# Attention scores for 512 queries and one key block at a time, in a fused Mamba and attention kernel

## The chip, the cores and the metric

The kernel runs on one core of a Trainium2 chip. The metric is the device time of one execution in microseconds. The core has five engines, each with an instruction queue of its own that runs in order: TensorE (PE; its weight loads are shown apart as PEld), VectorE (DVE), ScalarE (ACT), GpSimd (POOL) and SyncE (SP), which here issues the DMAs. Matmuls write into PSUM, which has eight banks of 512 f32 values in each of 128 partitions. GpSimd does not read PSUM in this kernel.

## The reference, cut to what matters

A conditioned state-space layer comes first and its result is added to x; then attention follows on x of shape (4, 1024, 512) with 16 heads of 32 channels. The change lies in the attention:

```python
q = heads(jnp.einsum('bsh,oh->bso', x, q_weight) * q_dc[:, None, :])
k = heads(jnp.einsum('bsh,oh->bso', x, k_weight) * k_dc[:, None, :])
v_flat = jnp.einsum('bsh,oh->bso', x, v_weight) * v_dc[:, None, :] * s2[:, None, :]
skip = v_flat
v = heads(v_flat)
attn = jnp.einsum('bhqd,bhkd->bhqk', q, k) * scale
attn = jax.nn.softmax(attn, axis=-1)
out = jnp.einsum('bhqk,bhkd->bhqd', attn, v).transpose(0, 2, 1, 3).reshape(B, S, H)
out = jnp.einsum('bsh,oh->bso', out, w_weight) * w_dc[:, None, :]
skip = jnp.einsum('bsh,oh->bso', skip, u_weight) * u_dc[:, None, :]
return out + skip
```

For every batch, head and query there are 1024 scores; their exponentials are summed (the denominator) and weight the values (the numerator), and the quotient goes through two projections.

## The kernel before

The state-space layer fills the first 1365 us of the span and the attention the rest. Attention is cut into 32 units (`NU`, line 1094): four batches, four groups of four heads, two halves of 512 queries. All 1024 keys of a unit's four heads lie in `ks` and its 512 queries in `qs`, with a 97th row that carries the negated maximum of each query's scores, so that the score matmul gives a number that can go straight into the exponential.

Work is written as small generators ("threads"), and `Loom` (line 44) is a planner: it keeps a clock for each engine, and each `yield` names an engine, an estimated duration and conditions. Whoever can start first is written next, with ties broken by a rank. The order it finds is fixed in each engine's queue by `Lane` (line 157). So the planner's estimates decide the order, and the chip's real durations decide how long each engine stands still within it. `Bins` (line 125) hands out buffers in the plan.

The threads that matter here, in one unit:

- `scores` (line 1152) runs over two halves of 256 queries (`qq`), four pairs of key blocks (`kp`) and four heads (`h`). Each step takes one of two PSUM banks (`sts`) and writes two matmuls of 128 keys by 256 queries, one for each key block of the pair.
- `exponent` (line 1165) is one ScalarE instruction over 128 x 512 values, into one of 12 SBUF buffers `p` (`PB`).
- `sums` (line 1184) adds the four `p` of a head and a query half: three additions of 512 columns, then a fold that adds the 256 columns of the second key block to those of the first. Head 1 does it on VectorE (`VADD`), the other three on GpSimd. There are four buffers `s` (`SB`).
- `groups` (line 1230) forms outputs: two groups for each query half, each with 16 matmuls (four key blocks, four heads), K of 128 keys, 32 output channels, 256 queries. Four heads go side by side into four column tiles of the array (`tile_position`) and into the 128 partitions of one of two banks `avs`, of which the outputs use the first 256 columns.
- `pay` (line 1206) sums over the partitions: four matmuls with a matrix of ones over the `s` of the four heads, 256 columns, into the other 256 columns of the same bank. It is written inside the next output group, or by `alone` (line 1225) when the planner comes to that first; a group that opens a query half has `due` of the owed sums among its conditions. A payment frees the four `s` buffers.
- `ratio` (line 1263): VectorE's reciprocal of the sums, then its product with the outputs, 256 queries at a time, and a store to DRAM (`aod`).

Beside these, `peaks` and `peak` (lines 1317 and 1330) find the maxima for the next unit (`dps`, `r`, `mps`), `heads` projects q and k (`qps`), `values` v (`vps`), and `skip`, `output` and `ending` do the last projections (`ups`, `ops`). They share the four common banks (`bank_of`, line 1119). `ending` (line 1652) handles the last batch's last four token blocks: three quarters of the projection are formed ahead, and the last quarter when `final` is there, which `ratio` sets for each query half of the last unit.

Of the kernel before, what the change touches and what calls it, by code (L numbers as in the profile page):

```python
# [8 lines left out]
F32 = mybir.dt.float32  # L9
# [3 lines left out]
ALU = mybir.AluOpType  # L13
# [22 lines left out]
AFTER = mybir.DependencyInfo(mybir.DependencyClass.Sync, mybir.DependencyReason.DATA)  # L36
# [811 lines left out]
PB = 12  # L848
SB = 4
# [5 lines left out]
LAT1 = {'PE': 0.3, 'ACT': 0.4, 'DVE': 0.8, 'POOL': 0.8, 'SP': 4.0, 'L1': 0.0}  # L855
EXTRA = {'PE': 0.1, 'ACT': 0.3, 'DVE': 0.3, 'POOL': 0.5, 'SP': 1.0}
MARGIN = 0.9
END = (12, 3, 12)
LAND = {"q": 5.5, "k": 9.0, "d": 10.5}
DUE = {'norm': (-206, 14.4), 'heads': (-96, 24), 'v0': (-108, 2.2), 'v1': (12, 2.2), 'skip': (100, 8), 'out': (266, 9)}  # L860
# [229 lines left out]
def attention(ctx, E, T, out, begun):  # L1090
    tc, nc, I, dc, x1d = E.tc, E.nc, E.I, E.dc, E.x1d
    NT = T // 128
    U = 8
    NU = B * U
# [4 lines left out]
    pm, pst, pav = (ep(tc.tile_pool(name="l1" + n, bufs=c, space=PSUM, reuse_waits="tile"))  # L1099
                    for n, c in (("m", 1), ("st", 2), ("av", 2)))  # L1100
# [64 lines left out]
    def exponent(u, qq, kp, h, i, st):  # L1165
        key = u, qq, kp, h
        yield "ACT", 0.54, prs
        j = prs.take()
        p = work("p", [128, 2, 256], PB)
# [5 lines left out]
        if kp == 1:  # L1175
            loom.add(sums(u, qq, h), place(u, qq, 1, h))
# [7 lines left out]
    def sums(u, qq, h):  # L1184

        eng = "DVE+" if h in VADD else "POOL"
        us, add = (0.62, dve) if h in VADD else (1.3, pool)
        s = None
        for kp in range(1, 4):
            yield (eng, us) + ((srs,) if s is None else ()) + (have("p", u, qq, kp, h),)  # L1190
            first = s is None
            if first:
                j, s = srs.take(), work("s", [128, 2, 256], SB)
            add.tensor_tensor(out=s, in0=P[u, qq, 0, h][1] if first else s, in1=P[u, qq, kp, h][1], op=ALU.add)
            for x in (0, 1) if first else (kp,):
                drop((u, qq, x, h))
# [9 lines left out]
    def pay(u, qq):  # L1206

        a = owed.pop((u, qq))
        for h in range(4):
            sm = pe.matmul(a[1][32 * h:32 * h + 32, 1, :], ones, S[u, qq, h][1][:, 0, :], start=True, stop=True, tile_position=(0, 32 * h))  # L1210
            if h == 0:
                for x in range(1, 4):
                    tc.add_manual_dep(sm.ins, S[u, qq, x][2], AFTER, reason="heads together")
        for h in range(4):
            srs.give(S.pop((u, qq, h))[0])
        loom.add(ratio(u, qq, *a), place(u, qq, 3, 3))

    def due(u, qq):

        def at():  # L1220
            ts = [done.get(("sum", u, qq, h)) for h in range(4)]
            return 0.0 if (u, qq) not in owed else None if None in ts else max(ts) + MARGIN
        return at

    def alone(u, qq):
        yield "PE", 0.8, due(u, qq)
        if (u, qq) in owed:
            pay(u, qq)

    def groups():  # L1230

        v = E.v
        for u, qq, kg in np.ndindex(NU, 2, 2):
            hg = u % U // 2
            names = [(u, qq, kp, h) for kp in (2 * kg, 2 * kg + 1) for h in range(4)]
# [3 lines left out]
            vs = [have("v", u // U, hg // 2, tb) for tb in range(4 * kg, 4 * kg + 4)]  # L1239
            yield ("PE", 2.05 + (0.41 if kg == 0 and owed else 0.0), *conds, *vs)  # L1240
            if kg == 0:
                ai = avs_of.take()
                a = ai, pav.tile([128, 2, 256], F32, tag="a", name="avs")
            for i in range(4):
                kb = 4 * kg + i
                for h in range(4):
                    c = hg * 128 + 32 * h
                    mm = pe.matmul(a[1][32 * h:32 * h + 32, 0, :], v[:, kb, c:c + 32], P[u, qq, 2 * kg + i // 2, h][1][:, i % 2, :],
                                   start=kb == 0, stop=kb == NT - 1, tile_position=(0, 32 * h))
                    if i == 0 and h == 0:  # L1250
# [12 lines left out]
    def ratio(u, qq, ai, a):  # L1263
# [8 lines left out]
        mark("av1", u, qq)  # L1272
        if u == NU - 1:
            final[qq] = ao
            mark("final", qq)
            return
        yield "SP", 0.6
        sp.dma_start(out=aod[b, hg, :, qh * 512 + qq * 256:qh * 512 + qq * 256 + 256], in_=ao)
        aos.give(j)
        mark("ao", b, hg, 2 * qh + qq)  # L1280

# [247 lines left out]
    def values(b, hf):  # L1529
        yield "SP", 0.01, past("skip", b - 1)  # L1530
        j, (wh, wl) = yield from weight("v", b, hf)
        free = [past("av", b * U - 1 - 4 * (1 - hf), 1)]
        for tb in range(NT):
            i = None
            for half in range(2):
                yield ("PE", 0.75) + ((bank_of, have("xs", b, tb), *free) if i is None else ())
                if i is None:
                    i, ps = bank([128, 256], "vps")
                for kb in (2 * half, 2 * half + 1):
                    for n, (a, ww) in enumerate(((E.xh, wh), (E.xh, wl), (E.xl, wh))):  # L1540
                        pe.matmul(ps, a[:, kb, tb * 128:tb * 128 + 128], ww[:, kb, :], start=kb == 0 and n == 0, stop=kb == 3 and n == 2)
            yield "ACT", 0.3
            acte.copy(E.v[:, tb, hf * 256:hf * 256 + 256], ps)
            bank_of.give(i)
            mark("v", b, hf, tb)
        whs.give(j)
        mark("values", b, hf)
# [104 lines left out]
    def ending(b, tb):  # L1652
# [133 lines left out]
```

## Time and profile before

| | |
|---|---|
| median of 3 runs | 2790.56 us (2787.77 to 2792.78) |
| profiled execution | 2796.49 us |
| its span, first to last instruction | 2794.7 us |
| attention, 1365 to 2775 us: PE, DVE, ACT, POOL busy | 1328.4, 951.4, 961.7, 1118.6 us |
| mean granted TensorE clock | 0.951 |
| exponentials (p<-st), 1024 instructions | 606 ns each |
| reciprocals, 64 instructions of 256 columns | 1755 ns each |
| recorded rows of outputs (avs<-p) and sums (avs<-s) | 4096 and 512 |

Busy time of PE is the union of its matmuls' durations. A matmul's duration includes its way through the array, so two that follow each other overlap in the record, and what one costs the queue is the distance from its start to the next start. The weight loads are a track of their own, since they run under the matmul before. An f32 matmul of the text appears as two rows. The clock switches between 1.0 and 0.5 in short stretches. All attention instructions carry line 167, the helper `Lane`; they are told apart by their tiles: `st` scores, `p` exponentials, `s` partial sums, `avs` outputs and sums, `ao` the quotient.

### The profile page before, as it was taken

To read this page: it belongs to the slowest core of one execution; us is meant where nothing else is said; L and a number is where in the kernel's file an instruction comes from. 1 tells how busy PE (TensorE), PEld (TensorE's weight loads), DVE (VectorE), ACT (ScalarE), POOL (GpSimd) and SP (SyncE) were. 2 spreads that over 40 slices of the span, in tenths; PEclk is the share of its full clock that TensorE was granted. 3 is DMA by queue.
4 is the path that set the end of the run, shared out by engine and by line. 5 is a ranking of instruction groups with operands and counts; after the bars stand their busy time and mean duration, and the time that the engine had idled before them with its cause. 6 is when DMAs were issued, how large, how long until landed. Compare 5 with 4: busy or idle time off the path is not lost.

```text
span 2794.7 us, 54619 instructions
## 1 busy us (share of the span) xinstructions
PE 2566.8 (92%) x18421; PEld 1775.8 (64%) x18421; DVE 1994.9 (71%) x3518; ACT 2021.2 (72%) x3766; POOL 2083.1 (75%) x2365
## 2 busy tenths in 40 slices
PE   7798999999999998886989899989999899999998
PEld 7565565665566665433756677756777667777765
DVE  4778888888878887674557766677567786667665
ACT  5888888888888888663567677667766676676674
POOL 5887788787778787443378888787787787777786
PEclk9899999999999999787989999999999999999998
DMA  5789989999989999895652455344553545345422
GB/s 173 226 239 273 271 267 274 274 265 272 270 250 272 273 276 266 254 252 147 174 130 82 121 141 171 104 127 116 147 144 118 135 124 140 120 121 151 107 58 91
DMA packets 333772, 518.26 MB, mean 185 GB/s; under 512 B 33514, under 2 KB 108586, under 8 KB 333362
## 3 DMA queue, kind: packets, MB, share of 16 engines
q1 hardware_dynamic: 333076, 514.71, 65.1%
q8 instruction: 145, 2.38, 0.4%
q14 instruction: 135, 1.11, 0.1%
q10 hardware_dynamic: 416, 0.07, 0.0%
HBM read 422.35 MB, written 92.05 MB: 184 GB/s over the span
## 4 chain that ended last, share of the span: by engine, by line
PE 43%; DMA 15%; POOL 15%; ACT 11%; DVE 8%; issue 7%; SPq 0%; ACTq 0%; POOLq 0%; DVEq 0%
DMA rep<-xnd 9%; PE avs L167 8%; PE st L167 7%; POOL s L167 5%; ACT u L167 5%; PE ups L167 5%; PE qps L167 4%; DVE g L167 4%; PE mps L167 3%; PE ps L167 3%; POOL tmp L167 3%; PE vps L167 3%; PE dps L167 3%; POOL tm L167 2%; PE po L167 2%
## 5 line engine op out<-in xcount | busy, mean ns | idle before, releaser
L167 DVE CUSTOM_DVE_ANT_0 g<-g,u,hi 128x512 f32<-128x512 f32 x1024 | 820.5, 801 | 209.4 <-ACT u L167 171.3
L167 ACT ACTIVATE p<-st 128x512 f32<-128x512 f32 x1024 | 599.2, 606 | 312.3 <-PE st L167 288.6
L167 ACT ACTIVATE u<-rep,bd 128x512 f32<-128x512 f32 x1024 | 699.4, 689 | 121.5 <-DMA rep<-xnd 67.8
L167 POOL TENSOR_TENSOR s<-s,p 128x512 f32<-128x512 f32 x384 | 538.9, 1420 | 58.1 <-ACT p L167 57.2
L167 DVE CUSTOM_DVE_ANT_0 r<-mps,r 128x512 f32<-128x512 f32 x496 | 334.7, 683 | 271.9 <-PE mps L167 249.7
L167 PE MATMUL ps<-xh,w_in 128*128 128x256 f32 x2048 | 493.4, 317 | 15.2 <-ACT w_in L167 10.5
L167 PE MATMUL st<-qs,ks 97*128 97x256 f32 x2048 | 450.5, 305 | 33.1 <-ACT p L167 24.0
L167 PEld LDWEIGHTS st<-qs,ks 97*128 97x128 f32 x2048 | 350.1, 195 | 152.4 <-ACT p L167 82.8
L167 POOL TENSOR_TENSOR s<-p 128x512 f32<-128x512 f32 x192 | 255.1, 1342 | 202.2 <-PE avs L167 106.9
L167 PEld LDWEIGHTS ps<-xh,w_in 128*128 128x128 f32 x2048 | 344.8, 191 | 91.7 <-issue 65.3
L167 PE MATMUL yb<-g,sy 128*32 128x512 f32 x2048 | 287.9, 633 | 57.7 <-DVE g L167 42.5
L167 ACT ACTIVATE r<-dps 128x512 f32<-128x512 f32 x496 | 298.5, 606 | 42.2 <-DVE m L167 20.5
L167 POOL TENSOR_TENSOR tmp<-tmp,tm 128x256 f32<-128x256 f32 x372 | 272.6, 733 | 73.6 <-ACT tmp L167 44.6
L167 PE MATMUL ps<-xl,w_in 128*128 128x256 f32 x1024 | 290.2, 283 | 0.0
L167 PE MATMUL avs<-p,v 128*32 128x256 f32 x4096 | 269.8, 408 | 2.4 <-ACT p L167 2.3
L167 PE MATMUL mps<-ks,qs 96*128 96x512 f32 x528 | 222.3, 435 | 16.1 <-DMA ks<-bnc 9.7
L167 PEld LDWEIGHTS ps<-xl,w_in 128*128 128x128 f32 x1024 | 196.4, 192 | 30.1 <-issue 30.1
L167 PE MATMUL dps<-ds,qs 96*128 96x512 f32 x496 | 204.4, 413 | 11.6 <-DMA bnc<-fh 5.7
L167 PEld LDWEIGHTS avs<-p,v 128*32 128x32 f32 x4096 | 126.8, 116 | 112.6 <-issue 25.4
L167 POOL TENSOR_SCALAR tm<-xr,c_w_conv 128x256 f32<-128x256 f32 x372 | 182.3, 490 | 20.1
L167 PE MATMUL qps<-xs,wqh 128*128 128x512 f32 x480 | 190.1, 401 | 0.1
L167 PE MATMUL ups<-wo,th 128*128 128x256 f32 x960 | 187.8, 288 | 0.0
(389 smaller groups left out, 4826.2 us busy)
## 6 DMA issues: line engine op xcount, KB each, us to landing
rep<-xnd SPq DMA_DIRECT2D x1024, 256.0 KB, 4.8
qs<-bnc SPq DMA_DIRECT2D x96, 256.0 KB, 4.5
ks<-bnc SPq DMA_DIRECT2D x96, 256.0 KB, 7.6
bnc<-fh SPq DMA_DIRECT2D x76, 256.0 KB, 3.3
bnc<-fl SPq DMA_DIRECT2D x76, 256.0 KB, 3.0
xnd<-z SPq DMA_DIRECT2D x64, 256.0 KB, 4.6
io<-x1d SPq DMA_DIRECT2D x57, 256.0 KB, 3.4
ds<-bnc SPq DMA_DIRECT2D x48, 256.0 KB, 9.0
```

The lines of the kernel that those rows point to most:

```text
L167: i = f(*a, **k)
```

## The change

A score step now takes all 512 queries and one key block: one matmul of 512 columns in place of two of 256. The exponentials keep their size and their number. A head of a unit has one chain of seven additions of 512 columns and no fold. An output group has two key blocks and four heads, 8 matmuls of 512 columns, and a unit has four groups that accumulate in one whole bank. The sums of a unit are four matmuls of 512 columns into one of the four common banks, always written by `alone`, with a rank four behind the unit's last step (`PAY`) where it was twelve, and the groups no longer wait for them. `ratio` takes the two query halves one after the other and gives the banks back behind the second. In the ending of the last batch, the last two token blocks are loaded only when the batch's first four are done. `srs`, `prs`, `aos` and the other buffers keep their number.

```diff
@@ scores, exponent
-    def place(u, qq=0, kp=0, h=0):
-        return 32 * u + 16 * qq + 4 * kp + h
+    def place(u, kb=0, h=0):
+        return 32 * u + 4 * kb + h
...
-            for qq, kp, h in np.ndindex(2, 4, 4):
+            for kb, h in np.ndindex(NT, 4):
                 yield "PE", 0.25, sts, have("row", u), have("k", u // 2, 0), have("k", u // 2, 1)
                 i = sts.take()
-                q, k = qs[u % 3], ks[u // 2 % 2]
-                st = pst.tile([128, 2, 256], F32, tag="t", name="st")
-                for e in range(2):
-                    kb = 2 * kp + e
-                    pe.matmul(st[:, e, :], k[0:97, h, kb * 128:kb * 128 + 128], q[0:97, h, qq * 256:qq * 256 + 256], start=True, stop=True)
-                loom.add(exponent(u, qq, kp, h, i, st), place(u, qq, kp, h))
+                st = pst.tile([128, 512], F32, tag="t", name="st")
+                pe.matmul(st, ks[u // 2 % 2][0:97, h, kb * 128:kb * 128 + 128], qs[u % 3][0:97, h, :], start=True, stop=True)
+                loom.add(exponent(u, kb, h, i, st), place(u, kb, h))
@@ sums
-        for kp in range(1, 4):
-            yield (eng, us) + ((srs,) if s is None else ()) + (have("p", u, qq, kp, h),)
+        for kb in range(1, NT):
+            yield (eng, us) + ((srs,) if s is None else ()) + (have("p", u, kb, h),)
...
-        yield eng, us * 0.55
-        i = add.tensor_tensor(out=s[:, 0, :], in0=s[:, 0, :], in1=s[:, 1, :], op=ALU.add)
-        S[u, qq, h] = j, s, i.ins.name
-        mark("sum", u, qq, h)
+        S[u, h] = j, s, i.ins.name
+        mark("sum", u, h)
@@ pay, alone
-        a = owed.pop((u, qq))
+        a = owed.pop(u)
+        n, sm = bank([128, 512], "sms")
         for h in range(4):
-            sm = pe.matmul(a[1][32 * h:32 * h + 32, 1, :], ones, S[u, qq, h][1][:, 0, :], start=True, stop=True, tile_position=(0, 32 * h))
+            i = pe.matmul(sm[32 * h:32 * h + 32, :], ones, S[u, h][1], start=True, stop=True, tile_position=(0, 32 * h))
...
-        yield "PE", 0.8, due(u, qq)
-        if (u, qq) in owed:
-            pay(u, qq)
+        yield "PE", 1.05, due(u), lambda: bank_of() if u in owed else 0.0
+        if u in owed:
+            pay(u)
@@ groups
-        for u, qq, kg in np.ndindex(NU, 2, 2):
+        for u, kg in np.ndindex(NU, 4):
...
             if kg == 0:
-                conds += [avs_of] + [due(*n) for n in owed]
...
-            yield ("PE", 2.05 + (0.41 if kg == 0 and owed else 0.0), *conds, *vs)
+                conds += [avs_of]
...
+            yield ("PE", 2.05, *conds, *vs)
...
-            for i in range(4):
-                kb = 4 * kg + i
+            for kb in (2 * kg, 2 * kg + 1):
                 for h in range(4):
                     c = hg * 128 + 32 * h
-                    mm = pe.matmul(a[1][32 * h:32 * h + 32, 0, :], v[:, kb, c:c + 32], P[u, qq, 2 * kg + i // 2, h][1][:, i % 2, :],
+                    mm = pe.matmul(a[1][32 * h:32 * h + 32, :], v[:, kb, c:c + 32], P[u, kb, h][1],
                                    start=kb == 0, stop=kb == NT - 1, tile_position=(0, 32 * h))
...
-            for n in list(owed):
-                pay(*n)
-            if kg == 1:
-                owed[u, qq] = a
-                mark("av", u, qq)
-                loom.add(alone(u, qq), place(u, qq, 3, 3) + 12)
+            if kg == 3:
+                owed[u] = a
+                mark("av", u)
+                loom.add(alone(u), place(u, 7, 3) + PAY)
@@ ratio
-        yield "DVE", 1.7, aos
-        j, ao = aos.take(), work("ao", [128, 256], 2)
-        dve.reciprocal(ao, a[:, 1, :])
-        yield "DVE", 0.35
-        dve.tensor_tensor(out=ao, in0=a[:, 0, :], in1=ao, op=ALU.mult)
-        avs_of.give(ai)
+        for qq in range(2):
+            c = slice(qq * 256, qq * 256 + 256)
+            yield "DVE", 1.7, aos
+            j, ao = aos.take(), work("ao", [128, 256], 2)
+            dve.reciprocal(ao, sm[:, c])
+            if qq:
+                bank_of.give(n)
+            yield "DVE", 0.35
+            dve.tensor_tensor(out=ao, in0=a[:, c], in1=ao, op=ALU.mult)
+            if qq:
+                avs_of.give(ai)
...
@@ ending
-        rs, ao, j, jo = yield from places(b, tb, *[have("ao", b, hg, tb // 2) for hg in range(3)])
+        rs, ao, j, jo = yield from places(b, tb, *[have("ao", b, hg, tb // 2) for hg in range(3)], *([have("out", b)] if tb > 5 else []))
```

More of the change, by code (lines that the diff above doesn't have):

```diff
@@ L857 @@
 MARGIN = 0.9
+PAY = 4
 END = (12, 3, 12)
@@ L1145, in parts, with exponent @@
         return j, tuple(work(x, [128, 512], 1, F32R, f"{x}{j}") for x in ("fh", "fl"))
-    def place(u, qq=0, kp=0, h=0):
-        return 32 * u + 16 * qq + 4 * kp + h
+    def place(u, kb=0, h=0):
+        return 32 * u + 4 * kb + h
     def scores():
         for u in range(NU):
-            for qq, kp, h in np.ndindex(2, 4, 4):
+            for kb, h in np.ndindex(NT, 4):
                 yield "PE", 0.25, sts, have("row", u), have("k", u // 2, 0), have("k", u // 2, 1)
                 i = sts.take()
-                q, k = qs[u % 3], ks[u // 2 % 2]
-                st = pst.tile([128, 2, 256], F32, tag="t", name="st")
-                for e in range(2):
-                    kb = 2 * kp + e
-                    pe.matmul(st[:, e, :], k[0:97, h, kb * 128:kb * 128 + 128], q[0:97, h, qq * 256:qq * 256 + 256], start=True, stop=True)
-                loom.add(exponent(u, qq, kp, h, i, st), place(u, qq, kp, h))
+                st = pst.tile([128, 512], F32, tag="t", name="st")
+                pe.matmul(st, ks[u // 2 % 2][0:97, h, kb * 128:kb * 128 + 128], qs[u % 3][0:97, h, :], start=True, stop=True)
+                loom.add(exponent(u, kb, h, i, st), place(u, kb, h))
             mark("scores", u)
-    def exponent(u, qq, kp, h, i, st):
-        key = u, qq, kp, h
+    def exponent(u, kb, h, i, st):
+        key = u, kb, h
         yield "ACT", 0.54, prs
         j = prs.take()
-        p = work("p", [128, 2, 256], PB)
+        p = work("p", [128, 512], PB)
         e = acte.activation(p, st, AF.Exp)
@@ L1174, in exponent @@
         mark("p", *key)
-        if kp == 1:
-            loom.add(sums(u, qq, h), place(u, qq, 1, h))
+        if kb == 1:
+            loom.add(sums(u, h), place(u, 1, h))
     def drop(key):
@@ L1182, in drop, with sums @@
             prs.free[P[key][0]] = (pleft.pop(key)[1], prs.k)
-    def sums(u, qq, h):
+    def sums(u, h):
         eng = "DVE+" if h in VADD else "POOL"
@@ L1188, in sums @@
         s = None
-        for kp in range(1, 4):
-            yield (eng, us) + ((srs,) if s is None else ()) + (have("p", u, qq, kp, h),)
+        for kb in range(1, NT):
+            yield (eng, us) + ((srs,) if s is None else ()) + (have("p", u, kb, h),)
             first = s is None
             if first:
[L1193 to L1196, printed above, removed]
@@ L1197, in sums @@
-        yield eng, us * 0.55
-        i = add.tensor_tensor(out=s[:, 0, :], in0=s[:, 0, :], in1=s[:, 1, :], op=ALU.add)
-        S[u, qq, h] = j, s, i.ins.name
-        mark("sum", u, qq, h)
+                j, s = srs.take(), work("s", [128, 512], SB)
+            i = add.tensor_tensor(out=s, in0=P[u, 0, h][1] if first else s, in1=P[u, kb, h][1], op=ALU.add)
+            for x in (0, 1) if first else (kb,):
+                drop((u, x, h))
+        S[u, h] = j, s, i.ins.name
+        mark("sum", u, h)
@@ L1202, in attention, with pay @@
     S = {}
     owed = {}
-    def pay(u, qq):
-        a = owed.pop((u, qq))
+    def pay(u):
+        a = owed.pop(u)
+        n, sm = bank([128, 512], "sms")
         for h in range(4):
-            sm = pe.matmul(a[1][32 * h:32 * h + 32, 1, :], ones, S[u, qq, h][1][:, 0, :], start=True, stop=True, tile_position=(0, 32 * h))
+            i = pe.matmul(sm[32 * h:32 * h + 32, :], ones, S[u, h][1], start=True, stop=True, tile_position=(0, 32 * h))
             if h == 0:
                 for x in range(1, 4):
-                    tc.add_manual_dep(sm.ins, S[u, qq, x][2], AFTER, reason="heads together")
+                    tc.add_manual_dep(i.ins, S[u, x][2], AFTER, reason="heads together")
@@ L1214, in pay, with due @@
         for h in range(4):
-            srs.give(S.pop((u, qq, h))[0])
-        loom.add(ratio(u, qq, *a), place(u, qq, 3, 3))
-    def due(u, qq):
+            srs.give(S.pop((u, h))[0])
+        loom.add(ratio(u, n, sm, *a), place(u, 7, 3))
+    def due(u):
         def at():
-            ts = [done.get(("sum", u, qq, h)) for h in range(4)]
-            return 0.0 if (u, qq) not in owed else None if None in ts else max(ts) + MARGIN
-        return at
-    def alone(u, qq):
-        yield "PE", 0.8, due(u, qq)
-        if (u, qq) in owed:
-            pay(u, qq)
+            ts = [done.get(("sum", u, h)) for h in range(4)]
+            return 0.0 if u not in owed else None if None in ts else max(ts) + MARGIN
+        return at
@@ L1230, in groups, with alone @@
+    def alone(u):
+        yield "PE", 1.05, due(u), lambda: bank_of() if u in owed else 0.0
+        if u in owed:
+            pay(u)
     def groups():
         v = E.v
-        for u, qq, kg in np.ndindex(NU, 2, 2):
+        for u, kg in np.ndindex(NU, 4):
             hg = u % U // 2
-            names = [(u, qq, kp, h) for kp in (2 * kg, 2 * kg + 1) for h in range(4)]
+            names = [(u, kb, h) for kb in (2 * kg, 2 * kg + 1) for h in range(4)]
             conds = [have("p", *n) for n in names]
@@ L1237, in groups @@
             if kg == 0:
-                conds += [avs_of] + [due(*n) for n in owed]
-            vs = [have("v", u // U, hg // 2, tb) for tb in range(4 * kg, 4 * kg + 4)]
-            yield ("PE", 2.05 + (0.41 if kg == 0 and owed else 0.0), *conds, *vs)
+                conds += [avs_of]
+            vs = [have("v", u // U, hg // 2, kb) for kb in (2 * kg, 2 * kg + 1)]
+            yield ("PE", 2.05, *conds, *vs)
             if kg == 0:
                 ai = avs_of.take()
-                a = ai, pav.tile([128, 2, 256], F32, tag="a", name="avs")
@@ L1244, in groups @@
-            for i in range(4):
-                kb = 4 * kg + i
+                a = ai, pav.tile([128, 512], F32, tag="a", name="avs")
+            for kb in (2 * kg, 2 * kg + 1):
                 for h in range(4):
                     c = hg * 128 + 32 * h
-                    mm = pe.matmul(a[1][32 * h:32 * h + 32, 0, :], v[:, kb, c:c + 32], P[u, qq, 2 * kg + i // 2, h][1][:, i % 2, :],
+                    mm = pe.matmul(a[1][32 * h:32 * h + 32, :], v[:, kb, c:c + 32], P[u, kb, h][1],
                                    start=kb == 0, stop=kb == NT - 1, tile_position=(0, 32 * h))
-                    if i == 0 and h == 0:
+                    if kb == 2 * kg and h == 0:
@@ L1253, in groups, with ratio @@
                 drop(n)
-            for n in list(owed):
-                pay(*n)
-            if kg == 1:
-                owed[u, qq] = a
-                mark("av", u, qq)
-                loom.add(alone(u, qq), place(u, qq, 3, 3) + 12)
+            if kg == 3:
+                owed[u] = a
+                mark("av", u)
+                loom.add(alone(u), place(u, 7, 3) + PAY)
     final = {}
-    def ratio(u, qq, ai, a):
+    def ratio(u, n, sm, ai, a):
         b, r = divmod(u, U)
         hg, qh = divmod(r, 2)
-        yield "DVE", 1.7, aos
-        j, ao = aos.take(), work("ao", [128, 256], 2)
-        dve.reciprocal(ao, a[:, 1, :])
-        yield "DVE", 0.35
-        dve.tensor_tensor(out=ao, in0=a[:, 0, :], in1=ao, op=ALU.mult)
-        avs_of.give(ai)
[L1272 to L1280, printed above, removed]
+        for qq in range(2):
[9 more added lines that the diff above has]
+                avs_of.give(ai)
+            if u == NU - 1:
+                final[qq] = ao
+                mark("final", qq)
+                continue
+            yield "SP", 0.6
+            sp.dma_start(out=aod[b, hg, :, qh * 512 + qq * 256:qh * 512 + qq * 256 + 256], in_=ao)
+            aos.give(j)
+            mark("ao", b, hg, 2 * qh + qq)
     def row(u, m1):
@@ L1531, in values @@
         j, (wh, wl) = yield from weight("v", b, hf)
-        free = [past("av", b * U - 1 - 4 * (1 - hf), 1)]
+        free = [past("av", b * U - 1 - 4 * (1 - hf))]
         for tb in range(NT):
```

## The prediction, made before the changed kernel was seen

> **What bounds the kernel now.** I read the page first: its totals and the chain of work that ended last.
>
> ```profile
> span 2794.7 us, 54619 instructions
> ...
> PE 2566.8 (92%) x18421; PEld 1775.8 (64%) x18421; DVE 1994.9 (71%) x3518; ACT 2021.2 (72%) x3766; POOL 2083.1 (75%) x2365
> ...
> DMA rep<-xnd 9%; PE avs L167 8%; PE st L167 7%; POOL s L167 5%; ACT u L167 5%; PE ups L167 5%; PE qps L167 4%; DVE g L167 4%; PE mps L167 3%; PE ps L167 3%; POOL tmp L167 3%; PE vps L167 3%; PE dps L167 3%; POOL tm L167 2%; PE po L167 2%
> ```
>
> The change lies in attention alone, so the second view is that stage (columns: length, then busy time and count of each engine, clock, DMA).
>
> ```profile
> 1365.00:2775.00 1410.00, 1328.40 (x10547) 991.28 (x10548) 951.43 (x1707) 961.70 (x1829) 1118.55 (x910) 0.95 0.45 123
> ```
>
> TensorE is busy for 1328.4 of 1410.0 us there and idle for 81.6; GpSimd for 1118.6 (79%). TensorE's queue is the bound, and the chain has GpSimd's additions (POOL s, 5% of the span, 140 us) as its second strand. So I price the change in time of TensorE's queue, by the distance from one start to the next where the queue is full.
>
> ```profile
> 1916.29 0.64 PE L167 MATMUL avs<-s,ones 128*32 128x256 f32 x8
> 1916.85 0.51 PE L167 MATMUL ups<-wo,th 128*128 128x256 f32 x2
> ...
> 1917.67 0.40 PE L167 MATMUL st<-qs,ks 97*128 97x256 f32 x2
> 1917.91 0.40 PE L167 MATMUL mps<-ks,qs 96*128 96x512 f32 x1
> 1918.14 0.40 PE L167 MATMUL ups<-wo,th 128*128 128x256 f32 x2
> ...
> 1920.40 1.93 PE L167 MATMUL avs<-p,v 128*32 128x256 f32 x32
> 1922.26 0.51 PE L167 MATMUL st<-qs,ks 97*128 97x256 f32 x2
> ```
>
> Each f32 matmul of the text is two instructions here (sums: 4 calls, 8 rows). A pair of 256-wide scores takes 0.24 us, a 512-wide mps 0.23, a group of outputs 1.86, the four sums 0.57. The weight loads do not show: they run under the matmul before.
>
> **The change, part by part.** *Scores*: 1024 pairs of 256 columns become 1024 single matmuls of 512. Over the stage's unblocked places a pair takes 0.24 to 0.25 us, and mps and dps, which have the same width and one row less, 0.23 to 0.24. That is 0 to 0.010 us each; I take 0.007, so 1024 x 0.007 = 7 us less (0 to 10). The Trainium skill ("TensorE: Matmul & The Clock Gate", section "Back-to-back issue gap") says that in a stream of loads and matmuls one of 512 columns settles at about 131 ns. By that the scores would give 1024 x 0.11 = 113 us. This trace has rows of just that form at 230 to 240 ns, and these decide.
>
> *Outputs*: 128 groups of 16 matmuls (32 rows) of 256 columns become 128 groups of 8 (16 rows) of 512. Nothing in attention has that form; the scan's yb does (K 128, 32 columns of weights, 512 wide, four column tiles).
>
> ```profile
> 601.19 0.16 PEld L167 LDWEIGHTS yb<-g,sy 128*32 128x32 f32 x8
> 602.19 0.19 PEld L167 LDWEIGHTS ps<-xh,w_in 128*128 128x128 f32 x1 [0.84 <-issue]
> ```
>
> Eight such rows take 1.00 us. For 256 columns 8 rows take 0.57 and 32 take 1.86, so each further 8 take (1.86 - 0.57) / 3 = 0.43 and a group starts with 0.14 us once. At 512 the first 8 take 1.00 = 0.14 + 0.86, the next 8 another 0.86: 1.86, what the group takes now. I count 0. If each 8 pays its 0.14 again, 2.00, it is 128 x 0.14 = 18 us more; if the 0.14 vanishes, 18 us less. Both ends go into the range.
>
> *Sums*: 64 payments of 8 rows at 256 become 32 of 8 rows at 512. A payment between other work costs 0.57 us, and some 0.19 more for changing over (in that stretch of the timeline a score pair ahead of a payment takes 0.33 instead of 0.24, 1934.69 to 1935.02, and the ups pair behind one 0.34, 1916.85 to 1917.19). 11 of the 64 stand beside an output group and cost only 0.43. Before: 53 x 0.76 + 11 x 0.43 = 45 us. After, all alone: 32 x (1.00 + 0.19) = 38. So 7 us less. Together TensorE's queue gets 14 us shorter at full clock; at the stage's mean clock of 0.95, 14.7.
>
> *Additions*: a head of one unit had two chains of three 512-wide additions and a 256-wide fold; now it has one chain of seven additions.
>
> ```profile
> L167 POOL TENSOR_TENSOR s<-s,p 128x512 f32<-128x512 f32 x384 | 538.9, 1420 | 58.1 <-ACT p L167 57.2
> L167 POOL TENSOR_TENSOR s<-p 128x512 f32<-128x512 f32 x192 | 255.1, 1342 | 202.2 <-PE avs L167 106.9 <-ACT p L167 83.8 <-PE mps L167 3.2
> L167 POOL TENSOR_TENSOR s<-s 128x256 f32<-128x256 f32 x192 | 163.4, 857 | 1.3
> ...
> L167 DVE TENSOR_TENSOR s<-s,p 128x512 f32<-128x512 f32 x128 | 137.4, 1074 | 27.3 <-ACT p L167 26.7
> L167 DVE TENSOR_TENSOR s<-p 128x512 f32<-128x512 f32 x64 | 69.8, 1090 | 2.7 <-ACT p L167 2.7
> L167 DVE TENSOR_TENSOR s<-s 128x256 f32<-128x256 f32 x64 | 63.5, 993 | 0.4
> ```
>
> GpSimd: 2 x (1.342 + 2 x 1.420 + 0.857) = 10.08 us a head, then 1.342 + 6 x 1.420 = 9.86: 0.22 x 96 = 21 us less. VectorE: 8.46, then 7.53: 0.93 x 32 = 30 us less. I cost both at nothing directly, since TensorE's work covers them; without that cover they would be worth at most these figures.
>
> *Waits for the sums*: TensorE stands still before the sum matmuls until the last addition is done, and everything planned behind them (scores, peaks, projections) waits with it. The second row is the other side: the next chain's first addition waits for its s buffer, which a payment frees.
>
> ```profile
> PE avs L167 <- POOL s L167: 12.3, 13, 2.1
> ...
> POOL s L167 <- PE avs L167: 106.9, 31, 12.2
> ```
>
> With 1.6 us behind VectorE's addition that is 13.9 us in 64 payments, 0.22 each. Half as many payments at the same wait: 7 us less. The output groups also stop waiting for the last sums; their own exponents cover that, so 0. *The ratio* stays two reciprocals (1.76 us each) and two products a unit, back to back, and still 62 stores of results, two at a unit's end instead of one per half; SP's queue has room at a 45% DMA share, so 0. *The bank* for the sums is new: held for about 1.0 + 0.7 + 1.76 + 0.42 + 1.76 = 5.6 us a unit, 32 x 5.6 = 180 of 4 x 1410 = 5640 us of banks, 3%. I count 0; a rival takes it up.
>
> *The end*: both halves of the last unit become ready together. Now the last sums start at 2784.25 and the last store is issued at 2791.67. Two folds go (1.85 us from 2782.35); the sum matmuls take 0.43 more, a second reciprocal with its product 2.18, two more closing steps 2 x (0.28 + 0.69) = 1.94 on VectorE: +2.7. The last two token blocks' loads now wait for the four earlier output blocks, whose matmuls today run on to 2787.9; if those stay there it costs a load, a split and 18 matmuls of 0.235, some 7 us more. I take +4 (2.7 to 10).
>
> Sum: -14.7 - 7 + 4 = -17.7 us of the profiled execution's 2794.7 us span, so 2777.0. That execution took 2796.5 in all (1.8 around the span), 5.9 above the median of the runs, 2790.56. From the median: 2772.9, and **2773** is the forecast.
>
> **The rivals.** *The sums come later than planned, slower.* The order of every queue is planned with 1.3 us for an addition and 0.715 for a fold. Per payment GpSimd falls behind by 3 x (5.04 - 4.615) = 1.27 us now, and by 3 x (9.86 - 9.1) = 2.3 with seven additions. If GpSimd never rests within a unit, each payment waits 0.22 + 1.03 = 1.25 us: 32 x 1.25 = 40 us instead of 13.9, so -14.7 + 4 + 26.1 = +15.4: 2806. It decides from (13.9 + 10.7) / 32 = 0.77 us a payment on. For it: one longer chain, four s buffers, GpSimd 79% busy. Against: it now waits 58.1 + 83.8 us for exponents, 4.4 a unit, which takes up the lateness.
>
> *More comes free.* The chain holds 140 us of POOL s, 2.2 per payment. With half the payments and no fold, a third of the 70 us could leave the path, the rest being covered by TensorE's work: -17.7 - 23 = -41, 2750. Against: only 81.6 us of TensorE idle is there, and most of it has other causes (ACT p 24.0).
>
> *The bank takes the gain.* If a peak pair waits 0.55 us a unit because one of four banks is out, 32 x 0.55 = 17.6: no change, 2790. Against: TensorE waits just 8.3 us in all for VectorE and ScalarE at mps and dps. A planned order that merely falls out differently belongs here too.
>
> *It does not do what it says*: I see no way; the shapes are in the text.
>
> **How the numbers follow.** Forecast 0.42 (2761 to 2785 by the bounds of its terms), more free 0.18, no change 0.12, late sums 0.28. This kernel's runs lie within 5 us, so 0.2% is about what can be told from no change. Faster by over 0.2%: 0.42 + 0.18 = 0.60; within: 0.12; slower: 0.28. The range runs from the freer rival to the slower one, with 18 us of output groups possible either way: 2748 to 2808.
>
> **What would show it.** Scores at 0.235 us from start to start; groups of 16 output rows at 1.86; 32 payments of 1.00; GpSimd's s rows at 96 x 7 = 672 of 512 columns and none of 256; waits before the sums under 10 us in all. I am wrong if those exceed 25 us, if the groups take 2.0, or if TensorE's idle time in the stage grows beyond 82 us for any cause, mps and dps waiting for banks first.

## The result and the profile after

The changed kernel takes 2829.99 us (median of 4 runs, 2825.45 to 2839.62) against 2791.67 us (4 runs, 2787.77 to 2796.30): a ratio of 1.0137 with a 95% interval of [1.0115, 1.0159]. That is 38 us slower where I had forecast 18 us less, and outside the range of 2748 to 2808 us. The profiled execution's span grew from 2794.7 to 2831.8 us. The page of the changed kernel, its span, totals and chain of waits:

```profile
span 2831.8 us, 47681 instructions
...
PE 2575.0 (91%) x15093; PEld 1614.7 (57%) x15093; DVE 1984.3 (70%) x3486; ACT 2019.1 (71%) x3766; POOL 2053.2 (73%) x2269
...
DMA rep<-xnd 10%; PE st L167 7%; PE avs L167 7%; PE qps L167 5%; PE ups L167 5%; ACT u L167 4%; PE ps L167 4%; DVE g L167 3%; PE mps L167 3%; POOL s L167 3%; PE vps L167 3%; PE dps L167 3%; POOL tmp L167 3%; PE yb L167 2%; PE po L167 2%
```

TensorE has 3328 matmul rows fewer. GpSimd's additions (POOL s), the second strand of the chain before, fell from 5% to 3% of the span. So the parts of the kernel that the change meant to lighten did get lighter. The timeline of TensorE in the middle of attention (columns: start, length, engine, operation, and idle time before it) shows the unit costs:

```profile
1916.01 1.06 PE L167 MATMUL sms<-s,ones 128*32 128x512 f32 x8 [0.28 <-POOL s L167]
1917.00 0.50 PE L167 MATMUL st<-qs,ks 97*128 97x512 f32 x1
...
1917.57 0.40 PE L167 MATMUL mps<-ks,qs 96*128 96x512 f32 x1
1917.80 0.40 PE L167 MATMUL st<-qs,ks 97*128 97x512 f32 x1
...
1919.26 0.40 PE L167 MATMUL st<-qs,ks 97*128 97x512 f32 x1
1919.49 0.40 PE L167 MATMUL ups<-wo,th 128*128 128x256 f32 x2
...
1923.12 1.92 PE L167 MATMUL avs<-p,v 128*32 128x512 f32 x16
1924.98 0.50 PE L167 MATMUL st<-qs,ks 97*128 97x512 f32 x1
```

From start to start the sums take 0.99 us, a group of outputs 1.86, the mps ahead of a score 0.23 and the score at 1919.26 also 0.23: the values of the forecast. Over all scores that another matmul follows at once, at full clock, the median distance is 0.238 us where a pair took 0.245; the mean did not fall (0.289 us, before 0.284). GpSimd's partial sums, in the groups view, are 672 additions of 512 columns and no fold:

```profile
L167 POOL TENSOR_TENSOR s<-s,p 128x512 f32<-128x512 f32 x576 | 791.1, 1397 | 136.2 <-ACT p L167 133.8
...
L167 POOL TENSOR_TENSOR s<-p 128x512 f32<-128x512 f32 x96 | 129.2, 1356 | 145.8 <-ACT p L167 135.2
```

The time went to idle time and to the end. The two rows below run from 1365 us to the end of the last exponential, first before and then after:

```profile
1365.00:2778.50 1413.50, 1331.39 (x10566) 993.68 (x10566) 954.07 (x1710) 964.74 (x1834) 1121.72 (x912) 0.95 0.45 123
```

```profile
1365.00:2791.00 1426.00, 1329.71 (x7229) 825.74 (x7227) 940.02 (x1670) 962.50 (x1831) 1095.96 (x819) 0.96 0.44 121
```

TensorE's idle time grew from 82.1 to 96.3 us. Its busy time fell by only 1.7 us, though 3328 rows are gone. Busy time is not the cost to the queue: a matmul stands in the record with 0.40 to 0.50 us, of which the next one in a full queue covers all but 0.24, so a queue that is held up for a moment between two matmuls still looks busy. How much of the time that is, no row here tells.

The waits of the changed kernel from 1365 to 2811 us (total us, times, longest), and below them those of the kernel before, from 1365 to 2775 us, that answer to them. The stretch of the changed kernel reaches 20 us into its end, which adds 0.9 us to the wait of avs for p and 0.5 us to that of the sums:

```profile
ACT r L167 <- PE dps L167: 37.4, 28, 3.9
PE st L167 <- ACT p L167: 34.5, 56, 8.3
PE avs L167 <- ACT p L167: 15.2, 18, 5.5
...
PE dps L167 <- DVE m L167: 12.2, 4, 3.8
POOL s L167 <- PE sms L167: 10.2, 5, 7.6
PE sms L167 <- POOL s L167: 9.2, 9, 2.2
```

```profile
PE st L167 <- ACT p L167: 23.5, 51, 3.6
ACT r L167 <- PE dps L167: 15.0, 13, 4.0
...
PE dps L167 <- DVE m L167: 2.3, 4, 1.2
PE avs L167 <- ACT p L167: 2.3, 9, 0.3
```

The waits for the sums fell as forecast: TensorE's before the sums from 13.9 us (with VectorE's share) to 9.2, GpSimd's for an s buffer from 106.9 to 10.2. But ScalarE now waits 37.4 us for the peaks' dps instead of 15.0, TensorE waits more at scores, outputs and dps, all of them work that stands later in the planned order than its readers would like. ScalarE's wait for scores (ACT p behind PE st) fell meanwhile, from 288.6 to 257.6 us up to the last exponential, so its longer wait for dps is a sign of another order and not a price by itself.

The end is a place of its own. In both kernels it begins with the last exponential. Timeline of the kernel before:

```profile
2777.89 0.60 ACT L167 ACTIVATE p<-st 128x512 f32<-128x512 f32 x1 [0.35 <-PE st L167]
2782.86 0.33 SPq L167 DMA_DIRECT2D out<-io  x1
...
2791.67 0.33 SPq L167 DMA_DIRECT2D out<-wl  x1
```

and of the changed kernel:

```profile
2790.44 0.59 ACT L167 ACTIVATE p<-st 128x512 f32<-128x512 f32 x1
...
2803.61 0.38 SPq L167 DMA_DIRECT2D io<-resd  x1
...
2808.05 0.79 PE L167 MATMUL ups<-wo,th 128*128 128x256 f32 x2 [5.62 <-ACT th L167]
...
2814.41 0.34 SPq L167 DMA_DIRECT2D out<-io  x1
2815.08 0.32 SPq L167 DMA_DIRECT2D wh<-resd  x1
...
2819.86 1.22 PE L167 MATMUL ops<-wo,fh 128*128 128x512 f32 x2 [6.21 <-ACT fh L167]
```

Before, 16.2 us lie between the last exponential's end (2778.5) and the span's end. After, it is 40.8 us (2791.0 to 2831.8), so 24.6 of the 37.1 us that the span grew, in one execution of each kernel. The fourth token block's projection cannot load until an ending gives back its `io` buffer (2803.61), its store is issued at 2814.41, and only then may the last two blocks load (2815.08); TensorE stands still for 5.62 and 6.21 us between these links. The rest, 12.5 us, came earlier: the last exponential ends that much later. Of these, 3.2 us lie ahead of the first exponential (1368.9 against 1365.7 us).

### The profile page after: what moved, and what is told of

Read it like the earlier page. It is cut to its first block, busy times and chain, and to the rows that moved or that the text cites. A ratio compares the mean times of both kernels' runs of the same rounds, so it can differ in the third digit from the quotient of the medians.

```text
span 2831.8 us, 47681 instructions
## 1 busy us (share of the span) xinstructions
PE 2575.0 (91%) x15093; PEld 1614.7 (57%) x15093; DVE 1984.3 (70%) x3486; ACT 2019.1 (71%) x3766; POOL 2053.2 (73%) x2269
## 4 chain that ended last, share of the span: by engine, by line
PE 47%; DMA 17%; ACT 11%; POOL 10%; DVE 8%; issue 6%; SPq 1%; POOLq 0%; ACTq 0%; DVEq 0%
DMA rep<-xnd 10%; PE st L167 7%; PE avs L167 7%; PE qps L167 5%; PE ups L167 5%; ACT u L167 4%; PE ps L167 4%; DVE g L167 3%; PE mps L167 3%; POOL s L167 3%; PE vps L167 3%; PE dps L167 3%; POOL tmp L167 3%; PE yb L167 2%; PE po L167 2%
## 5 line engine op out<-in xcount | busy, mean ns | idle before, releaser
L167 POOL TENSOR_TENSOR s<-s,p 128x512 f32<-128x512 f32 x576 | 791.1, 1397 | 136.2 <-ACT p L167 133.8
L167 ACT ACTIVATE p<-st 128x512 f32<-128x512 f32 x1024 | 595.1, 606 | 271.0 <-PE st L167 257.6
L167 PE MATMUL ps<-xh,w_in 128*128 128x256 f32 x2048 | 493.8, 317 | 14.9 <-ACT w_in L167 10.2
L167 PE MATMUL st<-qs,ks 97*128 97x512 f32 x1024 | 448.8, 445 | 43.4 <-ACT p L167 34.5
L167 ACT ACTIVATE r<-dps 128x512 f32<-128x512 f32 x496 | 298.8, 607 | 63.8 <-PE dps L167 37.4
L167 PEld LDWEIGHTS st<-qs,ks 97*128 97x128 f32 x1024 | 197.4, 194 | 210.1 <-ACT p L167 138.4
L167 PE MATMUL avs<-p,v 128*32 128x512 f32 x2048 | 268.2, 645 | 15.2 <-ACT p L167 15.2
L167 DVE TENSOR_TENSOR s<-s,p 128x512 f32<-128x512 f32 x192 | 228.9, 1192 | 38.6 <-ACT p L167 37.1
L167 POOL TENSOR_TENSOR s<-p 128x512 f32<-128x512 f32 x96 | 129.2, 1356 | 145.8 <-ACT p L167 135.2
L167 PEld LDWEIGHTS ups<-wo,th 128*128 128x128 f32 x960 | 164.5, 193 | 47.8 <-issue 20.8
```

The costliest lines, as they stand in the source:

```text
L167: i = f(*a, **k)
```

## The experiments

Each kernel was timed beside the kernel before, whose own median lay between 2786.2 and 2795.8 us in the five sets of runs, so the ratios are to be compared. "End" is the time from the last exponential to the span's end in the profiled execution; "hold" is the mean time per unit from the first sum matmul's start to the end of the last instruction that reads the common bank, from the traces. One profiled execution can lie far from its kernel's median: e2's took 2795.2 us and was the fastest of ten, e4's took 2816.8 and was among the slowest.

| kernel | median us (runs) | ratio to before | end us | hold us |
|---|---|---|---|---|
| changed kernel | 2830.0 (4) | 1.0137 [1.0115, 1.0159] | 40.8 | 7.9 |
| e1 guard on block 4 | 2827.9 (4) | 1.0113 [1.0053, 1.0173] | 30.8 | 7.9 |
| e2 before, guard alone | 2807.1 (10) | 1.0056 [1.0023, 1.0088] | 29.4 | none |
| e3 before, guard and bank | 2831.9 (4) | 1.0127 [1.0078, 1.0175] | 34.0 | 2 x 2.7 |
| e4 short hold, PAY 4 | 2798.8 (10) | 1.0032 [1.0003, 1.0062] | 26.3 | 2.0 |
| e5 PAY 8 | 2845.5 (4) | 1.0192 [1.0172, 1.0211] | 31.3 | 7.8 |
| e6 short hold, PAY 8 | 2833.6 (4) | 1.0157 [1.0114, 1.0201] | 26.0 | 2.3 |
| e7 short hold, PAY 0 | 2808.9 (5) | 1.0059 [1.0035, 1.0082] | 26.5 | 2.1 |
| e8 longer hold, PAY 4 | 2837.1 (4) | 1.0168 [1.0144, 1.0193] | 31.0 | 11.1 |
| e9 sums in avs, PAY 0 | 2804.6 (6) | 1.0058 [1.0035, 1.0081] | 25.4 | none |
| e10 PAY 0 | 2828.5 (4) | 1.0143 [1.0110, 1.0176] | 37.2 | 7.7 |
| e11 before, guard, three banks | 2849.7 (4) | 1.0225 [1.0194, 1.0257] | 34.1 | a whole bank |
| e12 before, rank 8 | 2807.7 (6) | 1.0073 [1.0047, 1.0099] | 16.4 | none |
| e13 before, rank 4 | 2805.5 (10) | 1.0039 [1.0021, 1.0057] | 16.2 | none |
| e14 before, rank -4 | 2825.6 (4) | 1.0103 [1.0064, 1.0143] | 16.2 | none |
| e15 sums in st, copied, PAY 4 | 2828.5 (4) | 1.0116 [1.0085, 1.0146] | 28.3 | none |
| e16 sums in avs, PAY 4 | 2811.2 (8) | 1.0051 [1.0029, 1.0073] | 26.7 | none |

My theory after the result (A): what costs is the sums' common bank, and the guard in the ending that this bank makes necessary. I put the guard in because the four endings might otherwise hold all four common banks with accumulators that wait for the last sums, while the sums wait for a bank; no run here leaves it out. The rival (B): the planned order fell out worse by chance, and any small edit would move the time as much.

**The guard.** e1 takes the changed kernel and lets the first of the last four blocks wait instead of the last two:

```diff
-*([have("out", b)] if tb > 5 else [])
+*([have("out", b)] if tb == 4 else [])
```

> The changed kernel, but in the ending the token block that waits for the first four output blocks is block 4 (which takes one of the two io buffers) instead of blocks 6 and 7. Theory A (the end: from the last exponential to the end of the span the changed kernel takes 40.8 us against 16.2 before, because that new wait and the io buffer put output blocks 3, 6 and 7 one behind the other): the end part falls to 16 to 24 us and the time to 2806 to 2814 us. Theory B (the loss is spread over all units by another planned order, and the end only shows it): the time stays within 6 us of 2830.

Theory A missed and B held: 2 us less, though the end is 10 us shorter. The last exponential ends 9.9 us later in e1's profile, so what the end gave up was lost ahead of it. e2 puts the guard of the changed kernel into the kernel before:

```diff
-*[have("ao", b, hg, tb // 2) for hg in range(3)])
+*[have("ao", b, hg, tb // 2) for hg in range(3)], *([have("out", b)] if tb > 5 else []))
```

> The kernel before with nothing but the new wait: the last two token blocks of the ending wait for the first four output blocks. Theory A: the end part grows from 16.2 to 30 to 40 us, the time to 2806 to 2816. Theory B: the end has room, 2790 to 2796.

0.56% slower, 16 us, with an interval from 0.23 to 0.88%. The timeline of e2's end shows the serial chain that the guard makes:

```profile
2763.26 0.60 ACT L167 ACTIVATE p<-st 128x512 f32<-128x512 f32 x1 [0.16 <-PE st L167]
...
2776.67 0.33 SPq L167 DMA_DIRECT2D out<-wqh  x1
2777.04 0.43 SPq L167 DMA_DIRECT2D wh<-resd  x1
...
2781.17 1.22 PE L167 MATMUL ops<-wo,fh 128*128 128x512 f32 x2 [5.26 <-ACT fh L167]
...
2790.24 0.34 SPq L167 DMA_DIRECT2D out<-wl  x1
```

In this execution, e2's fastest, the last exponential ends 14.6 us earlier than in the profile of before, so that the two spans are nearly equal (2793.2 and 2794.7 us); the 0.56% comes from all ten runs. The load stands right behind the store at 2776.67, the matmuls wait for it until 2781.17, and 9 us of matmuls and closing steps follow. Every kernel of this study without a guard has an end of 16.2 to 16.4 us, every one with a guard 25.4 to 40.8.

**The bank in the kernel before.** e3 is e2 with the sums of a query half (64 payments of 256 columns, as before) in a common bank:

```diff
+        n, sums_to = bank([128, 512], "sms")
...
-            sm = pe.matmul(a[1][32 * h:32 * h + 32, 1, :], ones, S[u, qq, h][1][:, 0, :], start=True, stop=True, tile_position=(0, 32 * h))
+            sm = pe.matmul(sums_to[32 * h:32 * h + 32, 0:256], ones, S[u, qq, h][1][:, 0, :], start=True, stop=True, tile_position=(0, 32 * h))
```

The bank goes back behind the reciprocal. A payment is still written inside the next output group or by `alone`, and both now wait in the plan for a free bank as well.

> The kernel before with that wait and with the sums in one of the four common banks (256 columns, 64 payments, everything else as before). Theory A (the bank is scarce: peaks wait for it): slower than the run with the wait alone by 12 to 40 us, and TensorE loses it before dps and mps. Theory B (banks have room): within 6 us of the run with the wait alone.

25 us above e2 by the medians, 0.71% by the ratios (20 us; the two intervals just overlap). Scores, outputs and additions are those of the kernel before, so the bank, the new condition and the order that comes with them cost this much without any wide matmul. TensorE's idle time before dps and mps grew from 15 to 27 us between the two profiles, as A had it, but in all up to the last exponential it grew by only 3 us.

**The hold, shortened.** e4, e6 and e7 let ScalarE copy the sums to SBUF at once:

```diff
+        yield "ACT", 0.54
+        sums = work("sums", [128, 512], 1)
+        acte.copy(sums, sm)
+        bank_of.give(n)
...
-            dve.reciprocal(ao, sm[:, c])
-            if qq:
-                bank_of.give(n)
+            dve.reciprocal(ao, sums[:, c])
```

All have the guard on block 4; e1, e5 and e10 are their counterparts without the copy, with `PAY` 4, 8 and 0.

> The changed kernel with the wait on block 4, and ScalarE copies the sums to SBUF at once (32 copies of 512 columns), so that the bank is held for about 2.5 us of a unit instead of 5.6. Theory A: the units end at least 8 us earlier than in the run with the wait on block 4 alone, and TensorE's waits before dps, mps and ups shrink. Theory B: no earlier, or later by up to 19 us for ScalarE's 32 x 0.6 us.

> The guard on block 4 as in e1, and PAY = 8: the sums' matmuls are placed four steps later in the plan; the common bank is held as long as in e1 (about 5.6 us a unit by the durations of its five instructions). Theory A, the price is the time that the sums hold a common bank: about e1's 2828 us, 2815 to 2845. Theory B, the order of the plan falls out differently with any small change, without regard to the bank: anywhere from 2795 to 2845, and a scatter of 15 us or more against e1 with this alone.

> PAY = 8 as in e5, and ScalarE copies the sums to SBUF, after which the bank goes back, so about 2.5 us a unit instead of 5.6, as in e4. Theory A: 15 to 35 us faster than e5, which is what e4 gained over e1 (29 us). Theory B: e4's gain belonged to that one order; here the difference from e5 lies between -12 and +12 us.

> Short hold as in e4, and PAY = 0: the sums' matmuls are placed right behind the unit's last step. Theory A: like e4's 2799 us, 2788 to 2805. Theory B: no relation to e4, 2785 to 2840.

> e1's kernel with PAY = 0 and the sums in a common bank that is held through both reciprocals: the counterpart of e7 (2808.9 us), which differs by the copy alone. Theory A: 12 to 30 us above e7, so 2821 to 2839, in line with the other two pairs (e4 29 us under e1, e6 12 us under e5). Theory B: 2795 to 2845 with no relation to e7; within 8 us of e7 would take the hold of the bank out of the explanation for this PAY.

The copy gains 0.81% at PAY 4, 0.35% at PAY 8 and 0.84% at PAY 0: 0.67% on average, 19 us, always the same sign. At PAY 8 it is less than theory A asked (12 us by the medians instead of 15 to 35) and just within B's 12; e5 and e7 themselves missed A's numbers by 0.5 and 4 us. TensorE's idle time before dps, mps and ups did not shrink from e1 to e4 (19 and 23 us), as A had said it would. PAY alone moves the time by 18 us (e5 against e1), which is B's doing. One row of the waits falls with the hold in all three pairs (37.6 to 20.5, 44.8 to 34.9, 53.7 to 18.6 us); here e10, then e7:

```profile
ACT r L167 <- PE dps L167: 53.7, 32, 3.9
```

```profile
ACT r L167 <- PE dps L167: 18.6, 15, 2.7
```

My reading is that the planner could give the peaks' dps a bank only later, and that ScalarE waits for them.

**The hold, lengthened, and a whole bank.** e8 is e1 with the bank given back behind the second store and a reading of one column; e11 is e2 with `Bins(loom, 3)` for the common banks:

```diff
+            if qq:
+                yield "DVE", 0.1, 3.0
+                dve.tensor_copy(out=work("hold", [128, 1], 1), in_=sm[:, 511:512])
+                bank_of.give(n)
```

> e1's kernel, but the bank of the sums goes back only behind the store of the second query half and a reading of one column of the bank by VectorE, by the plan some 4.9 us later, so about 10 us a unit instead of 5.6; the work itself grows by one instruction of one column a unit. Theory A: slower than e1's 2828 us, by 5 to 25 us (2833 to 2853); where e4 gained 29 us by a hold of 3 us less, a proportional price would be some 40 us more, but the planner goes round a bank that it knows to be out. Theory B: within 8 us of e1.

> The kernel before with the guard of the ending (e2, 2807 us) and three common banks instead of four, for the whole of attention; nothing else differs. It prices a whole bank. Theory A, banks are what the peaks and projections live on: 40 to 120 us above e2 (2847 to 2927). Theory B, the common banks have room (the 3% of my prediction): within 10 us of e2.

e8 is 0.55% above e1 (9 us by the medians; the intervals overlap), e11 1.69% above e2, 43 us by the medians. The same row of waits in e8 and in e11:

```profile
ACT r L167 <- PE dps L167: 56.9, 38, 3.6
```

```profile
ACT r L167 <- PE dps L167: 124.9, 102, 4.0
```

57 us with one bank out for 11.1 us a unit, 125 with one out for good; with all four there, 13.6 (e2) and 15.0 (before), but up to 38.0 in kernels below. TensorE's own idle time does not tell what a bank is worth: from the first to the last exponential it is 85.3 us in e2's profile and 86.6 in e11's, though that stretch is 45 us longer in e11.

**The sums elsewhere.** e9 and e16 put the sums into the second bank of the outputs, and the first output group of a unit waits until nothing is owed; e15 puts them into a bank of the scores, with the copy.

```diff
-        n, sm = bank([128, 512], "sms")
+        n, sm = avs_of.take(), pav.tile([128, 512], F32, tag="a", name="avs")
...
-                conds += [avs_of]
+                conds += [avs_of, lambda: None if owed else 0.0]
```

> e1's kernel with the sums in the second of the two banks of the outputs instead of a common bank, no copy, PAY = 0; the first output group of the next unit then waits until both are free. The four common banks are never taken by the sums. Theory A, the price is the common bank: peaks wait as in the kernel before (TensorE behind VectorE's m at dps 2 to 6 us where the changed kernel has 12.2) and the time is 2793 to 2812. Theory B, luck of the order or something in the wide scores and groups themselves: 2815 to 2845, like e1 and e5.

> e9 (2804.6 us) with PAY = 4 instead of 0: a second draw of its order, the sums again outside the common banks. Theory A (the bank): below e1's 2828 us, which has the same PAY, by 10 to 35 us, so 2793 to 2818. Theory B: 2820 to 2845.

> The changed kernel with the guard on block 4, PAY = 4, and the sums in one of the two banks of the scores, copied by ScalarE at once, so that this bank is out for some 2.5 us a unit; the common banks are never taken by the sums, and the output groups wait for nothing new. Theory C: at the level of before's neighbours, 2790 to 2812. If its scores stall for the lost bank, TensorE's waits for exponentials at st grow over the 31 us of e4 and the time is 2812 to 2840.

e9 is 0.85% below e10 and e16 0.62% below e1, each with the same PAY: 0.74% on average, 20 us, for not taking a common bank, with twice the demand on the outputs' banks. Both lie in the range of A. e9's own expectation at dps was wrong (12.9 us, not 2 to 6), so the waits at dps are not where the gain shows; nor does ScalarE's row follow here, with 26.8 us in e9 and 34.1 in e16. e15 fits neither line: its waits at the scores are 30.1 us, no more than in e4, and yet it takes 2828.5 us. It takes no common bank, has the guard and the copy, and costs as much as e1: by itself it speaks against A. It may be one bad draw of an order; no run here decides.

**The order alone.** e12, e13 and e14 are the kernel before with one rank changed to 8, 4 and -4:

```diff
-                loom.add(alone(u, qq), place(u, qq, 3, 3) + 12)
+                loom.add(alone(u, qq), place(u, qq, 3, 3) + 8)
```

> The kernel before with one rank changed: a lone payment stands eight steps behind its unit half instead of twelve. No work and no bank differs; the planned order falls out differently. It shows how far the order alone moves the time. Theory A: within 10 us of before (2784 to 2804). Theory B: off by 10 us or more, in either direction, and then no single difference of that size between two kernels of this study says anything of its edit.

> The kernel before with the rank of a lone payment at 4 instead of 12, nothing else: a second draw of its order. Theory C, before's own order is a favourable draw and its neighbours lie some 10 to 20 us higher, as e12 did: 2796 to 2812. Theory D, e12 was the odd one and the remaining loss of the changed kernel is in its wide form: within 8 us of before (2784 to 2800).

> As e13 with the rank at -4, a third draw. Theory C: 2796 to 2815. Theory D: 2784 to 2800.

No work, bank or buffer differs, and they are slower by 0.73%, 0.39% and 1.03%: 0.72% on average, 20 us. So the order of the kernel before is better than these three neighbours. e12 went as its theory B had it, e14 even beyond the 2815 us of theory C: a single difference of some 20 us between two kernels of this study says nothing of its edit by itself, and only pairs that agree count. Whether the old order was a favourable draw, or 12 simply a better rank than any lower one, is open: all three lower the same rank, and no higher one and no edit elsewhere was tried. It also limits what the row above proves: in e13, where no bank is taken,

```profile
ACT r L167 <- PE dps L167: 38.0, 26, 3.5
```

The row shows that peaks stand late in the order; a missing bank is one cause of it, a worse draw another.

## Why the prediction was wrong

**The account.** The forecast was 17.7 us less, the profiled executions differ by 37.1 us more. Up to the last exponential TensorE's busy time fell by 1.7 us, where the queue's term said 14.7; its idle time there grew by 14.2, where I had 7 less; the end grew by 24.6, where I had 4. So the shorter queue hardly showed as less busy time (the 7 us of the scores stand in the median distance and not in the mean), the waits went the other way, and the end was six times its term. Each figure is of one execution of each kernel.

**Right.** The unit costs: scores (0.238 us in the median), output groups (1.86), sums (0.99), 672 additions without a fold, the waits before the sums (9.2 us, 4.7 less, where I had 7 less). The rival "the sums come later than planned", which I held for the likeliest way to a slower kernel, did not happen: it needed 0.77 us for each of the 32 payments and got 0.29. So the kernel was slower for other reasons than my slower case. The lines that I had named as proof against me were the right ones: TensorE's idle time passed 82 us, and its wait for VectorE and ScalarE at mps and dps, which I had read as 8.3 us, grew to 16.4, though scores and outputs took more of it. One reading of mine was off: 14 of the 64 payments stood beside an output group, not 11, which moves the sums' term by 1 us.

**Wrong: the bank for the sums, "held for about" 5.6 us a unit, 3% of the banks: "I count 0".** Two failures. The sum of 5.6 took the two reciprocals as back to back. VectorE's timeline in the changed kernel:

```profile
1918.24 1.74 DVE L167 RECIPROCAL ao<-sms 128x256 f32<-128x256 f32 x1
1919.91 0.62 DVE L167 CUSTOM_DVE_ANT_0 r<-mps,r 128x512 f32<-128x512 f32 x1
...
1920.46 0.41 DVE L167 TENSOR_TENSOR ao<-avs,ao 128x256 f32<-128x256 f32 x1
1920.80 0.68 DVE L167 TENSOR_TENSOR s<-p 128x512 f32<-128x512 f32 x1
1921.40 1.75 DVE L167 RECIPROCAL ao<-sms 128x256 f32<-128x256 f32 x1
```

Other work is queued between them, and the bank that was taken at 1916.01 is out until 1923.15. The mean over the units is 7.9 us, up to 13. The larger failure is the share: an average occupancy of 3% says nothing of what the peaks and projections lose when one of their four banks is out, in one piece, once a unit. Shortening the hold from 7.8 to 2.2 us brings 19 us, doing without the bank 20 us, each an average of two or three pairs that agree in sign. The order alone moves a kernel by as much, and e15 does not fit, so a price near 20 us is likely and not proven. The rival "the bank takes the gain" had the right place and 17.6 us as its price; I gave it 0.12 because TensorE waited just 8.3 us for VectorE and ScalarE at mps and dps. That was the wrong row to ask: three banks instead of four (e11) cost 43 us and left TensorE's idle time where it was. My explanation, which the runs do not settle, is that a planned order hides the lack of a bank, since the planner puts the work later and nobody waits where the bank is missing.

**Wrong: "The end: +4 (2.7 to 10)".** It was +24.6 us in the profiled executions, and the guard alone gives +13.2 there (16.2 to 29.4) and 0.56% of the time. I added a load, a split and 18 matmuls on the condition that the fourth block's matmuls stay where they were. They did not: in the changed kernel that block itself waits for a buffer that an ending holds, and so three links, each with a load and its matmuls, follow one another.

**Missing: the draw of the order.** I named it in half a sentence under a rival. It is a term of its own: an edit to the plan gives up this kernel's order for another, and three others cost 11, 20 and 29 us by their ratios. My 0.2% for what can be told from no change was too fine for the same reason.

**The sum.** In shares of the time: -0.78 for the forecast without its +4 us at the end, +0.56 for the guard, +0.7 for the bank, +0.72 for an ordinary order, in all +1.2, where 1.37 +/- 0.22 was measured. The parts are not independent, and the order scatters by about as much as each of them (e1, e5 and e10, which differ in PAY alone, lie at 1.0113, 1.0192 and 1.0143), so the agreement is no proof of each, and how the loss divides among them stays open. What the wide forms themselves gain was not measured alone. From their first to their last exponential the two kernels with the sums in avs take 1416.7 and 1415.4 us, and before's three neighbours 1416.8, 1425.8 and 1438.4, 1427 on average: 11 us less, where TensorE's and the waits' terms promised 21.7. But before itself takes 1412.8 us and e2 1400.2, each figure is one execution, and e12's and e13's lay 11 us below and 14 us above their medians. A gain of the wide forms is not shown. No variant that I ran beats the kernel before; the nearest is e4, at 1.0032.

## What to carry to other kernels

Price a shared bank by how long it is out and who is queued on its reader's engine meanwhile, not by its average share; and before its holder does slow work with it (here 2 x 1.75 us of reciprocal), copy it out: 0.6 us a unit on ScalarE went with 12 to 29 us less by the medians of three pairs. A condition added to the last steps of a kernel makes a chain of load, matmuls and store with nothing left to hide it; look at the time from the last exponential on, not at the whole. And where a planner writes the order, draw the order of the old kernel a few times too before the difference of two kernels is put down to the edit.

## What the runs showed of the hardware that I had not expected

After its waits in the changed kernel's end TensorE comes back at half clock. The windows (length, busy time and count of each engine, granted clock, DMA):

```profile
2808.00:2813.00 5.00, 4.95 (x21) 4.72 (x22) 0.69 (x1) 0.00 (x0) 0.00 (x0) 0.50 0.00 0
...
2819.80:2823.70 3.90, 3.84 (x9) 3.04 (x10) 1.32 (x3) 0.72 (x3) 0.00 (x0) 0.52 0.01 2
2823.70:2829.00 5.30, 4.14 (x16) 2.55 (x14) 1.58 (x3) 0.30 (x1) 0.00 (x0) 1.00 0.13 49
```

The projection behind the 5.62 us wait runs almost whole at 0.50, that behind the 6.21 us wait for its first 4 us, so each link of the serial end costs more than its matmuls' usual time. It is not the end alone: between 1365 us and the last exponential TensorE waits for longer than 4 us four times in the kernel before and three times in the changed one, and each time the first 2 us behind the wait are at 0.50. And executions of one and the same kernel spread more than the three runs shown at first: 2795.2 to 2832.6 us over ten runs of e2, 2782.9 to 2813.1 over nineteen of the kernel before.
